# Layer 0, first block: GpSimd normalises ten of the eleven parts of x, and the zero fills of u come after its last part

## The chip, the cores and the metric

The kernel runs on one NeuronCore of a Trainium2 chip. The metric is the device time of one execution in microseconds; the time given for a kernel is the median of its runs. Engines are named as the profile names them: PE (TensorE matmuls), PEld (its weight loads), DVE (VectorE), ACT (ScalarE), POOL (GpSimd) and SP (SyncE, which here only issues DMAs). `L470` is line 470 of the kernel's source.

## The reference

Four residual layers follow one another on x of shape 4 x 64 x 256 x 256 (batch, channels, rows, columns), all in float32: `x = x + conv(group_norm(x))`. Only layer 0 is touched by the change:

```python
def _L0_conv_ref(x, w_in, w_dw, fft_filter, w_out):
    x = jnp.einsum('bchw,oc->bohw', x, w_in)
    ...
    xf = jnp.fft.rfft2(xp) * fft_filter
    xp = jnp.fft.irfft2(xf, s=(p, p))
    ...
    x = lax.conv_general_dilated(x, w_dw, window_strides=(1, 1), padding=[(1, 1), (1, 1)], feature_group_count=C)
    x1, x2 = jnp.split(x, 2, axis=1)
    x = jax.nn.gelu(x1, approximate=False) * x2
    return jnp.einsum('bchw,oc->bohw', x, w_out)
...
x = x + _L0_conv_ref(_gn(x), L0_conv_w_in, L0_conv_w_dw, L0_conv_fft_filter, L0_conv_w_out)
```

`_gn` is a group norm with 32 groups of two channels, so that a normalised value is `r * x + nb` with one r and one nb for each channel and image. `w_in` widens 64 channels to 384; the FFT filter acts in patches of 8 x 8; the depthwise convolution has zero padding at the image's edge; `w_out` brings 192 gated channels back to 64.

## The kernel before

**Blocks and parts.** Layer 0 goes through 12 blocks, three to an image, each with 11 rows of patches (`blocks`, `NR`). A row of patches of x is loaded as two parts of 128 partitions x 1024 elements (four image rows each); the last row of block 0 is loaded as a single part of the same size that holds all eight image rows. So block 0 has 11 parts, `first_parts[0]` to `first_parts[10]`. The first ten are already in SBUF when the statistics are done, because they are the last ten tiles over which the statistics of image 0 run (`kept`); part 10 is loaded afterwards (L424), into a buffer that a normalised part sets free.

**Before the first block.** PE builds small tables, DVE expands them (`tables`), ACT and POOL copy them into the tiles T (L390), and POOL stores T to DRAM as the weights wt (L394). In the same time DVE takes the statistics of image 0 (L317), and `group_norm` turns them into r and nb (L197 to L218, the power on POOL at L217). The tile u is then allocated in the memory of a pool that held T, so whatever writes u first has to wait until the stores of T have landed.

**Normalising a part** (`normalize_x`, L429): either ACT does it (`normalize`, L253) or POOL (`tensor_scalar`, L441). In every block but the first it is ACT alone.

**A block.** It has four rounds `kb` of 48 channels. A round first runs `expand` (L459) for each step: 16 matmuls (32 records in the profile, since each float32 matmul shows as two) multiply a row or half rows of x with `win` into two PSUM tiles, and these are copied to u by ACT (the first tile) and DVE (the second), four copies each in the form that round 0 uses (L486). There are four such PSUM tiles, so two steps are in flight. Block 0 has 11 steps. A step reads all eight image rows of its patches, so steps 2j and 2j+1 need parts 2j and 2j+1; step 10 needs part 10. After the steps, the round runs its convolution and patch filter as matmuls on u (`own` L523 and `beside` L539), then Gelu on ACT (L546), the product on DVE (L547) and a store to DRAM from POOL (L550).

**Zeros.** u has cells outside the image. `clear_sides` (L729) fills two edge columns, two inner columns and a tail with zeros; the loop at L765 fills the row above the image in block 0 (and a row in the other blocks at an image's edge). All of them are POOL memsets; no copy of `expand` writes the same cells, and the matmuls of `own` and `beside` read them.

**Order of the work.** Within layer 0 the order on PE, DVE, ACT and SP is that of the source (`manual_schedule`, L677); POOL is not in that list, and the order of its instructions is decided by the planner. In block 0, round 0, the source normalises parts 0 to 3 ahead of step 0 and then one part ahead of each of the steps 1 to 7 (L793 to L795), odd parts on POOL and even ones on ACT. The planner's order on POOL before is: power L217, memset L767 (the row of zeros), parts 1, 3, 5, the five memsets of `clear_sides`, parts 7 and 9, and then the stores of L550. On ACT before, parts 0 and 2 stand ahead of the copies of step 0, and parts 4, 6, 8 and 10 stand between the copies of the steps. SP's order is: the loads of the first weights (L498), part 10 (L424), one more weight, and then x of image 1 for its statistics (L668).

Of the kernel before, what the change touches and what calls it, by code (L numbers as in the profile page):

```python
# [13 lines left out]
ALU = mybir.AluOpType  # L14
# [104 lines left out]
class _Net:  # L119
# [152 lines left out]
    def _layer0(self, ctx, dst):  # L272
        tc, nc, a, B, H, W = self.tc, self.nc, self.a, self.B, self.H, self.W
        pool = lambda name, bufs, **k: ctx.enter_context(tc.tile_pool(name=name, bufs=bufs, **k))
# [11 lines left out]
        HC = W // P // 2 + 1  # L286
        CW = 2 * HC
# [4 lines left out]
        NR = 11  # L292
# [118 lines left out]
        def parts_of(p):  # L411

            b, i0 = blocks[p]
            out = [(b, i0 + 1 + 2 * m, k) for m in range(NR // 2) for k in range(2)]
            return out + ([(b, i0 + NR, 2)] if i0 + NR < NP else [])
# [13 lines left out]
        def normalize_x(part, pool=False):  # L429
            b, i, k = part  # L430
            x = x0.pop(part).rearrange("p r w -> p (r w)")
            if k == 2:
                xns[b, i] = p_x1.tile([128, HW2 // P, P, P], F32, tag="x1", name=f"xn_{b}_{i}")
            elif k == 0:
                xns[b, i] = p_xn.tile([128, W // P, P, P], F32, tag="xn", name=f"xn_{b}_{i}")
            to = xns[b, i].rearrange("p m r w -> p r m w")
            if k < 2:
                to = to[:, 4 * k : 4 * k + 4]
            x = x.rearrange("p (r m w) -> p r m w", r=P if k == 2 else 4, w=P)
            if pool:  # L440
                nc.gpsimd.tensor_scalar(to, x, self.r[0][:, b : b + 1], self.nb[0][:, b : b + 1], ALU.mult, ALU.add)  # L441
            else:
                self.normalize(to, x, 0, b)

# [3 lines left out]
        E1, O1, O2, E2 = 0, HC, 1, HC  # L448

        def steps_of(p):  # L450

            b, i0 = blocks[p]
            one = lambda t: [(b, i0 + t, 0, [(t, 0), (t, 1)])] if 0 <= i0 + t < NP else []
            out = one(0)
            for t in range(1, NR, 2):
                out += [(b, i0 + t, q, [(t, q), (t + 1, q)]) for q in range(2)]
            return out + one(NR)
# [146 lines left out]
        def load_half(p, r, half):  # L604
            if 0 <= p < NB and r < P:
                if half == 0 and (p, r) not in rts:
                    load_r(p, r)
                load_g(p, r, half)
# [73 lines left out]
        with ordered:  # L682

            bst0 = new_bst0(0)
            first_parts = parts_of(0)
# [35 lines left out]
            u = None  # L721
            ctx_u = ExitStack()
            u = ctx_u.enter_context(tc.tile_pool(name="l0u", bufs=1))
            u = u.tile([128, PB, (NR + 1) * CW + 2], F32, name="u")
            sources = []
            rows_u = u[:, :, 0 : (NR + 1) * CW].rearrange("p c (t w) -> p c t w", w=CW)
            lo, hi = halves

            def clear_sides():  # L729

                nc.gpsimd.memset(rows_u[lo, :, :, E1], 0.0)
                nc.gpsimd.memset(rows_u[lo, :, :, O1 + HC - 1], 0.0)
                nc.gpsimd.memset(rows_u[hi, :, :, 0], 0.0)
                nc.gpsimd.memset(rows_u[hi, :, :, E2], 0.0)
                nc.gpsimd.memset(u[:, :, (NR + 1) * CW :], 0.0)

            for p in range(NB + 1):
                units = iter([(r, half) for r in range(P) for half in range(2)] if p > 0 else [])
                ahead, first = 1, []
                if p == NB:  # L740
                    ctx_u.close()
                    sources.append([pool("l0g1e", 6), pool("l0g6e", 6), pool("l0re", 3)])
                    ahead = 3
                for r in range(ahead):
                    for half in range(2):
                        first.append((p - 1, r, half))
                        if p == NB:
                            load_half(*first.pop())

                def unit():  # L750
                    at = next(units, None)
                    if at:
                        project(p - 1, *at)
                        load_half(p - 1, at[0] + ahead, at[1])

                if p == NB:
                    for k in range(2 * P):
                        unit()
                    while self.norms:
                        self.next_norms()  # L760
                    break
                b, i0 = blocks[p]
                fresh = parts_of(p + 1) if p + 1 < NB else []
                steps = steps_of(p)
                for t in (0, NR):  # L765
                    if not 0 <= i0 + t < NP:
                        nc.gpsimd.memset(rows_u[:, :, t], 0.0)  # L767
                nk = [] if b + 1 >= B else list(range(p % NI * NJ // NI, (p % NI + 1) * NJ // NI))
                loaded, begun, coming = [], iter(fresh), iter(fresh)

                def load_next(kb):
                    if kb == 3:
                        load_rows(2)
                    elif nk:
                        loaded.append(nk.pop(0))
                        load_stats(b + 1, loaded[-1])

                def load_rows(n):
                    for _, row in zip(range(n), begun):
                        load_x(row)  # L780

                def normalize_rows(n):
                    for _, row in zip(range(n), coming):
                        normalize_x(row)
                    load_rows(n)

                for kb in range(4):
                    for t in range(NR + 1):
                        if p == 0 and kb == 0:
                            if t == 1:  # L790
                                for part in first_parts[len(kept) :]:
                                    load_x(part)
                            for n in range(4) if t == 0 else range(t + 3, t + 4):  # L793
                                if n < len(first_parts):
                                    normalize_x(first_parts[n], pool=n % 2 == 1)  # L795
                        if t < len(steps):
                            expand(p, kb, steps[t], kb == 0 or t < (NR + 1) // 2)
                        if t in (0, 4) and first:
                            load_half(*first.pop(0))
                        if t == NR:  # L800
                            load_w(p * (HID // 8) + NG * kb // 2 + 3)
                            load_next(kb)
                    if p == 0 and kb == 0:
                        clear_sides()
                        ctx_f.close()
                        p_1, p_6 = (pool(n, 2, side="right") for n in ("l0g1", "l0g6"))
                        sources.append([p_1, p_6, pool("l0r", 2, side="right")])
                    for g in range(0, NG, 2):
                        if g > 0:
                            load_w(p * (HID // 8) + (NG * kb + g) // 2 + 3)  # L810
                        if g in (0, 2, 6, 8):
                            unit()
                        if g < 6 and kb < 3:
                            load_next(kb)
                        if kb == 3 and g == 0:
                            assert not self.norms
                            normalize_rows(3)
                        for k in range(2):
                            own(p, kb, g + k)
                        for k in range(2):  # L820
                            beside(p, kb, g + k)
                        if g < NG - 2 or kb == 2:
                            self.next_norms()
                        if kb == 3:
                            normalize_rows(2)
                            if p == NB - 1 and g < 2 * (NR // 2):
                                load_r(p, g // 2)
                            continue
                        if loaded:
                            next_stats(b + 1, loaded.pop(0))  # L830
                        if kb == 2 and g == NG - 2:
                            load_rows(2)
                for t in range(NR):
                    xns.pop((b, i0 + t), None)
# [728 lines left out]
```

## Time and profile before

| | us |
|---|---|
| runs of the kernel before | 6346.17, 6347.42, 6354.44 |
| median | 6347.42 |
| the profiled execution's own time | 6345.01 |
| its span, first to last instruction | 6343.0 |
| ACT, 17 normalisations of 128 x 1024 up to 365 us (L253) | 1.224 to 1.242 each |
| POOL, 5 normalisations of 128 x 1024 (L441) | 1.184 to 1.199 each |
| POOL, memset of the row of zeros (L767) | 1.467 |
| POOL, memsets of `clear_sides` (L731 to L735) | 1.116, 1.197, 1.143, 1.192, 0.197 |
| ACT copy to u, round 0 of block 0 (L486, 44 of them) | 0.482 to 0.532 |
| DVE copy to u, the same round (44 of them) | 0.549 to 0.564 |

Times inside the profile are counted from the start of its span. A line of the timeline gives the start, the duration, engine, source line, operation and tiles, how many instructions are merged in it, and in brackets how long the engine was idle just before and what ended that. Lines of one engine can be merged over short gaps. Engines run side by side, so a busy engine matters only where another one waits for it. A line of the waits gives who waited for whom, in total, how often, and the longest. The chain is followed back from the last instruction through whatever released each step.

### The profile page before, as it was taken

What the parts mean: (1) busy time and instruction counts of PE and PEld (TensorE: products, weight loads), DVE (VectorE), ACT (ScalarE), POOL (GpSimd) and SP (SyncE); (2) the same over time, 40 slices, a digit from 0 to 9 for tenths busy, and PEclk for the clock granted to TensorE, in tenths of its full rate; (3) what the DMA queues carried; (4) which work ended last, traced back from release to release, by engine and by line L of the source; (5) the groups of instructions that cost most, each with busy time, mean ns of one, the idle gap of its engine ahead of it and who ended that gap; (6) DMA issues with size and microseconds to landing.
All of it is one profiled execution on the core that took longest, in us unless ns stands there. A gap on an engine that the chain in (4) does not pass through costs nothing.

```text
span 6343.0 us, 233229 instructions
## 1 busy us (share of the span) xinstructions
PE 5965.4 (94%) x104150; PEld 3328.8 (52%) x104150; DVE 4315.4 (68%) x6003; ACT 3274.7 (52%) x4639; POOL 1054.2 (17%) x1651
## 2 busy tenths in 40 slices
PE   3999999999999999999999969999899999999987
PEld 2565655566665655556665533333344444443566
DVE  6566666666666666656665549999788988984265
ACT  4454444445454444344544407777777777772111
POOL 4111111111111111111111111111122222221011
PEclk9999999999999999999999979999999999999755
DMA  7477888887887878887768799999566666678799
GB/s 221 157 209 220 241 240 248 244 235 228 239 234 225 239 231 241 235 249 207 219 200 224 217 239 246 227 230 225 136 175 174 175 173 176 175 189 292 290 374 393
DMA packets 769595, 1441.98 MB, mean 227 GB/s; under 512 B 77412, under 2 KB 463476, under 8 KB 766548
## 3 DMA queue, kind: packets, MB, share of 16 engines
q1 hardware_dynamic: 616388, 917.72, 54.7%
q0 software_dynamic: 148672, 500.14, 23.5%
q8 instruction: 823, 13.48, 0.9%
q10 hardware_dynamic: 3536, 9.20, 0.6%
q14 instruction: 176, 1.44, 0.1%
HBM read 926.71 MB, written 500.04 MB: 225 GB/s over the span
## 4 chain that ended last, share of the span: by engine, by line
PE 83%; DVE 6%; DMA 6%; ACT 3%; issue 2%; POOL 0%; SPq 0%; ACTq 0%; POOLq 0%; DVEq 0%
PE pc L539 18%; PE pc L523 12%; PE m L946 10%; PE one L1187 9%; PE psu L470 8%; PE div L1146 7%; PE po L632 4%; DVE u L486 4%; PE psu L476 3%; PE psz L1176 2%; PE po L639 2%; ACT u L486 2%; PE psy L1521 2%; PE psa L1374 2%; DMA x<-x 2%
## 5 line engine op out<-in xcount | busy, mean ns | idle before, releaser
L547 DVE TENSOR_TENSOR h<-h,pc 128x374 f32<-128x374 f32 x1152 | 575.4, 541 | 1168.8 <-ACT h L546 1168.8
L546 ACT ACTIVATE h<-pc 128x374 f32<-128x374 f32 x1152 | 493.4, 480 | 1682.3 <-PE pc L539 1682.3
L539 PE MATMUL pc<-u,w 64*16 64x374 f32 (+2 forms) x27648 | 1178.0, 479 | 4.7 <-issue 4.5
L550 POOL DMA_DIRECT2D g<-h x576 | 415.5, 721 | 2834.5 <-DVE h L547 2724.2
L523 PE MATMUL pc<-u,w 64*64 64x374 f32 x9216 | 832.0, 484 | 10.1 <-DVE u L490 3.4
L486 DVE COPY u<-psu 64x384 f32<-64x384 f32 x1408 | 782.3, 556 | 60.4 <-PE psu L470 36.4
L539 PEld LDWEIGHTS pc<-u,w 64*16 64x16 f32 (+2 forms) x27648 | 465.5, 92 | 682.0 <-issue 645.4
L470 PE MATMUL psu<-win,xn 64*128 64x96 f32 x11264 | 759.9, 277 | 47.7 <-ACT u L486 26.7
L486 ACT COPY u<-psu 64x384 f32<-64x384 f32 x1408 | 722.8, 513 | 128.2 <-PE psu L470 100.8
L470 PEld LDWEIGHTS psu<-win,xn 64*128 64x128 f32 x11264 | 714.4, 188 | 114.3 <-ACT u L486 36.2
L1132 DVE TENSOR_TENSOR q<-xn 128x2313 f32<-128x2313 f32 (+2 forms) x256 | 628.0, 2495 | 1.7 <-ACT xn L253 1.7
L1187 PE MATMUL one<-z,wp 32*32 32x512 f32 x16384 | 598.1, 598 | 18.7 <-issue 14.9
L253 ACT ACTIVATE xn<-x,nb,r 128x1024 f32<-128x1024 f32 (+3 forms) x267 | 475.3, 1802 | 179.2 <-DMA x<-r 117.8
L523 PEld LDWEIGHTS pc<-u,w 64*64 64x64 f32 x9216 | 363.9, 132 | 383.5 <-issue 159.1
L1133 ACT ACTIVATE q<-q 128x2313 f32<-128x2313 f32 (+2 forms) x256 | 529.2, 2087 | 31.4 <-DVE q L1132 30.3
L1187 PEld LDWEIGHTS one<-z,wp 32*32 32x32 f32 x16384 | 368.7, 103 | 228.2 <-issue 87.7
L1146 PE MATMUL div<-q,ones 64*32 64x512 f32 x8192 | 465.9, 596 | 11.1 <-ACT q L1133 9.5
L1220 POOL DMA_DIRECT2D x<-r x512 | 274.5, 544 | 974.7 <-DVE r L1217 959.5
L476 PE MATMUL psu<-win,xn 64*64 64x96 f32 x12288 | 345.6, 250 | 39.9 <-issue 18.4
L632 PE MATMUL po<-g,wo 128*64 128x176 f32 (+1 forms) x3072 | 315.2, 348 | 45.0 <-DMA g<-g 36.9
L476 PEld LDWEIGHTS psu<-win,xn 64*64 64x64 f32 x12288 | 299.8, 135 | 82.3 <-issue 34.5
L946 PE MATMUL m<-t,wk 64*64 64x512 f32 x3072 | 341.1, 588 | 0.0
(157 smaller groups left out, 6428.7 us busy)
## 6 DMA issues: line engine op xcount, KB each, us to landing
g<-h POOLq DMA_DIRECT2D x576, 374.0 KB, 6.7
x<-x SPq DMA_DIRECT2D x240, 640.0 KB, 6.5
w<-wt SPq DMA_DIRECT2D x288, 448.0 KB, 6.9
x<-x SPq DMA_DIRECT2D x100, 1024.0 KB, 14.1
g<-g SPq DMA_DIRECT2D x414, 187.0 KB, 6.4
g<-g SPq DMA_DIRECT2D x736, 93.5 KB, 6.0
x<-in_x_dram SPq DMA_DIRECT2D x256, 256.0 KB, 8.0
x<-o POOLq DMA_DIRECT2D x128, 512.0 KB, 8.3
```

Of the source, the lines that this page charges most:

```text
L470: nc.tensor.matmul(ps[s][:, k, at], xn[halves[s], n : n + 2].rearrange("p n r w -> p (n r w)"), win[halves[s], kb, 0 : 2 * PB], start=True ...
L476: nc.tensor.matmul(ps[s][halves[1 - odd], k, at], xn[halves[s], n + odd].rearrange("p r w -> p (r w)"), win[halves[s], kb, PB * (1 - odd) ...
L486: copy(at(h, o0 + o), v[k, c : c + PB])
L523: nc.tensor.matmul(out(C * c, C, k, h), w[halves[h], k, 2 * (G % 2) + c, 0:C], cells(h, 4 * g + 2 * k + c, 0, 0), start=True, stop=False, ...
L539: nc.tensor.matmul(out(q, m, k, h), w[halves[h], k, 2 * (G % 2) + c, c0 : c0 + m], cells(h, 4 * g + 2 * k + c, down, right), start=False, ...
L547: nc.vector.tensor_mul(h[:, k], h[:, k], ps[k][:, 1, 0:L])
L632: nc.tensor.matmul(out(k, s, x), wo1, moving(g1[:, 2 * k], 2 * half + k, s, x), start=(x == 0), stop=False, skip_group_check=True,)
L946: nc.tensor.matmul(rows2(m)[halves[j], s], w[dx][halves[s]], ts[n][halves[s], i, 2 * j : 2 * j + 2, dx : dx + W], start=(dx == 0), stop=(d ...
L1132: nc.vector.tensor_sub(d, p0, p1)
L1133: nc.scalar.activation(d, d, AF.Square)
L1146: ins = nc.tensor.matmul(ps[quarters[j], h], ones[halves[h]], q[n, g, k][halves[h], r + 2 * j : r + 2 * j + 2, o : o + W], start=(m == 0), ...
L1187: ins = nc.tensor.matmul(rows2(ps[g])[quarters[j], k], w[quarters[i]], z[quarters[i], h, 2 * j + dy : 2 * j + dy + 2, dx : dx + W], tile_p ...
```

## The change

In block 0, round 0, POOL normalises parts 1 to 10 and ACT only part 0; they are still called in the same order from the same places. `normalize_x` hands back the POOL instruction. The row of zeros of block 0 is no longer filled at the head of the block: it joins the fills of `clear_sides` after round 0's steps, and each of these six memsets gets an added dependency on the last POOL normalisation, that of part 10. In the other blocks the row fills stay where they were.

The planner's order on POOL is then: power L217, parts 1 to 10 in turn, the memset of the row, the tail, the four columns, and then the stores. ACT's instructions lose parts 2, 4, 6, 8 and 10 and keep their order otherwise. The orders on PE, DVE and SP are as before. The buffer for part 10 is one that POOL's normalisations set free, where it was ACT's before; the loads of L668 follow with the other buffers. PE's step 10 waits for POOL as well, and PE's first matmul of `own` waits for POOL's memsets.

```diff
--- before.py
+++ after.py
@@ -438,7 +438,7 @@
                 to = to[:, 4 * k : 4 * k + 4]
             x = x.rearrange("p (r m w) -> p r m w", r=P if k == 2 else 4, w=P)
             if pool:
-                nc.gpsimd.tensor_scalar(to, x, self.r[0][:, b : b + 1], self.nb[0][:, b : b + 1], ALU.mult, ALU.add)
+                return nc.gpsimd.tensor_scalar(to, x, self.r[0][:, b : b + 1], self.nb[0][:, b : b + 1], ALU.mult, ALU.add)
             else:
                 self.normalize(to, x, 0, b)
 
@@ -728,11 +728,8 @@
 
             def clear_sides():
 
-                nc.gpsimd.memset(rows_u[lo, :, :, E1], 0.0)
-                nc.gpsimd.memset(rows_u[lo, :, :, O1 + HC - 1], 0.0)
-                nc.gpsimd.memset(rows_u[hi, :, :, 0], 0.0)
-                nc.gpsimd.memset(rows_u[hi, :, :, E2], 0.0)
-                nc.gpsimd.memset(u[:, :, (NR + 1) * CW :], 0.0)
+                at = [rows_u[lo, :, :, E1], rows_u[lo, :, :, O1 + HC - 1], rows_u[hi, :, :, 0], rows_u[hi, :, :, E2]]
+                return [nc.gpsimd.memset(v, 0.0) for v in at + [u[:, :, (NR + 1) * CW :]]]
 
             for p in range(NB + 1):
                 units = iter([(r, half) for r in range(P) for half in range(2)] if p > 0 else [])
@@ -762,11 +759,18 @@
                 b, i0 = blocks[p]
                 fresh = parts_of(p + 1) if p + 1 < NB else []
                 steps = steps_of(p)
+                zero_rows = []
                 for t in (0, NR):
                     if not 0 <= i0 + t < NP:
-                        nc.gpsimd.memset(rows_u[:, :, t], 0.0)
+                        zero_rows.append(t)
                 nk = [] if b + 1 >= B else list(range(p % NI * NJ // NI, (p % NI + 1) * NJ // NI))
                 loaded, begun, coming = [], iter(fresh), iter(fresh)
+
+                def clear_rows():
+                    return [nc.gpsimd.memset(rows_u[:, :, t], 0.0) for t in zero_rows]
+
+                if p > 0:
+                    clear_rows()
 
                 def load_next(kb):
                     if kb == 3:
@@ -792,7 +796,7 @@
                                     load_x(part)
                             for n in range(4) if t == 0 else range(t + 3, t + 4):
                                 if n < len(first_parts):
-                                    normalize_x(first_parts[n], pool=n % 2 == 1)
+                                    last = normalize_x(first_parts[n], pool=n > 0)
                         if t < len(steps):
                             expand(p, kb, steps[t], kb == 0 or t < (NR + 1) // 2)
                         if t in (0, 4) and first:
@@ -801,7 +805,8 @@
                             load_w(p * (HID // 8) + NG * kb // 2 + 3)
                             load_next(kb)
                     if p == 0 and kb == 0:
-                        clear_sides()
+                        for ins in clear_rows() + clear_sides():
+                            self.after(ins, last)
                         ctx_f.close()
                         p_1, p_6 = (pool(n, 2, side="right") for n in ("l0g1", "l0g6"))
                         sources.append([p_1, p_6, pool("l0r", 2, side="right")])
```

## The prediction

> **What bounds the kernel now.** I read the page first, then the timeline of the first 145 us, where all of block 0's round 0 lies, then the waits there and the same stretch in block 1. Over the whole span PE is the busy engine:
>
> ```profile
> PE 5965.4 (94%) x104150; PEld 3328.8 (52%) x104150; DVE 4315.4 (68%) x6003; ACT 3274.7 (52%) x4639; POOL 1054.2 (17%) x1651
> ```
>
> The edit touches one of the few places where PE is not busy. The timeline shows two losses there, a late start and a slow pace:
>
> ```profile
> 100.13 2.37 ACT L253 ACTIVATE xn<-x,nb,r 128x1024 f32<-128x1024 f32 x2 [18.59 <-DVE nb L218]
> 104.34 1.47 POOL L767 MEMSET u<- 128x1632 f32 x1 [4.43 <-DMA w<-wt]
> 105.80 3.54 POOL L441 TENSOR_SCALAR xn<-x,r,nb 128x1024 f32<-128x1024 f32 x3
> 107.04 5.62 PE L470 MATMUL psu<-win,xn 64*128 64x96 f32 x64 [7.98 <-POOL xn L441]
> 110.90 6.85 DVE L486 COPY u<-psu 64x384 f32<-64x384 f32 x12 [10.80 <-PE psu L470]
> ...
> 114.26 4.27 ACT L486 COPY u<-psu 64x384 f32<-64x384 f32 x8
> 118.56 1.24 ACT L253 ACTIVATE xn<-x,nb,r 128x1024 f32<-128x1024 f32 x1
> 118.57 4.56 DVE L486 COPY u<-psu 64x384 f32<-64x384 f32 x8 [0.82 <-PE psu L470]
> 119.83 4.27 ACT L486 COPY u<-psu 64x384 f32<-64x384 f32 x8
> 124.12 1.24 ACT L253 ACTIVATE xn<-x,nb,r 128x1024 f32<-128x1024 f32 x1
> 124.14 4.56 DVE L486 COPY u<-psu 64x384 f32<-64x384 f32 x8 [1.00 <-PE psu L470]
> ...
> 135.22 4.60 DVE L486 COPY u<-psu 64x384 f32<-64x384 f32 x8 [0.96 <-PE psu L470]
> ```
>
> The start: r and nb are known at 100.10 and ACT begins part 0 at once, but POOL's queue has the row memset in front of part 1, and that memset stands until 104.34 for a transfer. Part 1 starts at 105.80, and PE's first step at 107.04. The chain names the transfer as the last store of T, issued at 89.52 and landed 14.46 us later, at 103.98; the timeline's "w<-wt" is only what landed last by its guess.
>
> The pace: on ACT, eight copies (two steps) and one normalisation alternate, 118.56 to 124.12, 5.56 us for two steps. DVE is idle 0.8 to 1.0 us in each such pair, and PE waits for ACT. What the pace is without normalisations is seen in block 1, round 0, whose ACT has only copies: the DVE copies of the last 11 of its 12 steps are one line without a gap.
>
> ```profile
> 380.73 25.24 DVE L486 COPY u<-psu 64x384 f32<-64x384 f32 x44 [0.21 <-PE psu L470]
> ```
>
> That is 25.24 / 11 = 2.295 us a step, set by four DVE copies.
>
> Whether an earlier PE start is worth anything depends on when u's memory is free. The copies themselves wait for the stores of T too; the queue's own record of ACT says when that was over:
>
> ```profile
> L486 ACTq EVENT_SEMAPHORE  x1: 6528/6528/6528, 104.3 to 104.3; - x1
> ```
>
> At 104.3 ACT had passed all earlier waits of its first copy and stood 6.5 us longer for the last, PE. So the stores free u for everybody at about 104.35, not only for POOL.
>
> What follows is PE alone:
>
> ```profile
> 139.40:180.00 40.60, 40.60 (x766) 17.12 (x768) 16.18 (x31) 10.73 (x25) 7.46 (x11) 1.00 0.56 179
> ```
>
> From 139.4 to 180 PE (first pair of numbers) is busy for the whole 40.60 us. What is gained ahead of it moves it all.
>
> [...] 1.187 us on POOL against 1.240 on ACT for one part. [...] The DVE copies read PSUM; all 44 take 0.549 to 0.564 us, those beside POOL's two normalisations at 113.90 to 116.28 included. [...] step 0's 32 records take 3.78 us, a later step's 2.1. PE starts cold after the change too.
>
> **The change, part by part.**
>
> *Start.* Part 1 becomes POOL's first work after the power: from about 100.15 to 101.34. ACT's part 0 is the first half of the 2.37 us, to 101.37. PE then starts at 101.42, with the 0.05 us that it took before (part 1 ended at 106.99), which is 107.04 - 101.42 = 5.6 us earlier. Step 0 cold takes 3.8 us, so the first copies can start at 105.2, after u is free (104.35, 0.85 us to spare). Before it was 110.84 on ACT, 110.90 on DVE.
>
> *Pace.* Five normalisations leave ACT: part 2, which stood ahead of the steps and hid under the wait for part 1 (nothing), and parts 4, 6, 8, 10 at 1.24 us each. ACT's four copies take 2.13 us a step, DVE's 2.28, so DVE now sets the pace, 2.295 as in block 1. The eleven steps took 139.82 - 110.90 = 28.92 us from DVE's first copy to the end of its last; now 25.24. Gain 3.7 us, less than 4 x 1.24 = 4.96, because DVE is late next. Sum: 5.6 + 3.7 = 9.3 us, with DVE's last copy at 105.25 + 25.24 = 130.5 in place of 139.82.
>
> *POOL's load.* Ten parts at 1.187 us run from 100.15 to 112.0. Step 2j needs part 2j+1: part 3 at 103.7 for a step 2 that starts at about 107.5, part 9 at 110.8 for step 8 at about 121, and the margin grows. Part 10's load is issued once a POOL part frees its buffer, at 101.4 (ACT's part 0 freed one then); its two halves landed 5.5 to 6.1 us after issue, by 108.2, before POOL reaches it. If the buffer is part 3's it is 2.3 us later, and still in time. On SP only one weight and the loads of L668 stand behind it; those had waited until 107.01 for POOL's part 1 and can come sooner, and no engine waits for them before 147.
>
> *Zero fills.* Six memsets, 1.47 + 1.12 + 1.20 + 1.14 + 1.19 + 0.20 = 6.3 us, now follow part 10, from 112.0 to 118.4, or 119 with the waits. Their added wait is on POOL's own last normalisation; behind them are only POOL's stores, the first of which follows a product of DVE at about 136. Who needs them is `own` on PE at 137.34 - 9.3 = 128.0. Nine us of cover; once used up, each further us costs one.
>
> *Table load and the rest.* ACT's 1.28 us table load for Gelu at 139.44 stays hidden under `own` and moves with it.
>
> The profiled execution took 6345.01 for a span of 6343.0; its span should become 6333.7. The median of the runs is 2.4 above its time; from the median, 6347.42 - 9.3 = 6338.1, that is 0.15% less. 0.2%, 12.7 us, is about what a measurement of this kernel can tell from no change, so this counts as within it.
>
> **Unknowns.** [...] warm at once would bring the copies to 104.35 and save 0.9 more; cold through step 1 costs about 1[...]. So 8.3 to 10.2, with 9.3 as the same 3.8 us again. A slow landing of T's last store eats the start: from 105.2 on, one for one. Carrying through the other 6200 us I take as full: nothing in them depends on a fixed moment.
>
> **Rivals.**
> - *The start is held by the stores of T instead.* A transfer wait takes the place of POOL's. It decides past 105.2, 1.2 us later than the landing seen, and at 110.8 nothing of the 5.6 us is left: 6347.42 - 3.7 = 6343.7. For it: the DMA engines were 99% busy from 100 to 107. Against: nothing ahead of 101 is changed.
> - *Only the start gains*, because something other than ACT keeps the pace at 2.78: 6341.8. Block 1 speaks against it.
> - *Slower: the zero fills end last.* POOL's ten normalisations in a row could be slower than five in two groups. With t for each, the fills end at 106.9 + 10 t; they delay `own` from t = 2.1 us (128.0), cancel the gain at 3.0, and make the kernel 0.2% slower at t = 4.3, 6360.1. For it: everything is in one in-order queue. Against: 1.184 to 1.199 with DVE idle and with DVE busy.
> - *The gain is larger than 0.2%*: 9.3 us and 3.5 more, from the spread of two medians (the runs of before span 8.3 us) or from later waits that the shift closes; about 6333. Nothing in the profile points to such a wait.
>
> **Chances.** Forecast 0.67, stores 0.06, only the start 0.05, larger 0.17, slower fills and the like 0.05. Medians scatter by some 3 us, so of the forecast's cases about a tenth pass 12.7 us. Faster 0.24, within 0.70, slower 0.06. Range: 6331 to 6345, from the larger gain to the partial ones.
>
> **What would show it.** Right: POOL's part 1 at 100.2 and PE's first step at 101.4; DVE's 44 copies of round 0 as a nearly gapless line from 105.2 to 130.5; POOL's last memset before 120; `own` at 128; the span at about 6334. Wrong: PE waiting for POOL at a later step or at `own`; copies that start with T's stores and not with PE; POOL normalisations far above 1.2 us; or the 9.3 us present at 180 us and gone later.

## The result, and the profile after

| | before | after |
|---|---|---|
| median, us | 6347.11 (22 runs) | 6336.16 (22 runs) |
| lowest and highest, us | 6334.0 and 6356.99 | 6328.53 and 6349.62 |
| ratio, with its 95% interval | | 0.9985 (0.9979 to 0.9992) |
| span of the profiled execution, us | 6343.0 | 6346.7 |

The change makes the kernel 0.15% faster (0.08 to 0.21%), 9.5 us by the ratio (the two medians of the table lie 10.95 us apart, inside the same interval of 5 to 13); the forecast was 9.3 and 6338.1. The profiled execution of the changed kernel is one of its longer ones (own time 6348.79 against a median of 6336.16), so the two spans say nothing on the change. What it did is read in its stage, the first 140 us. The timeline of the changed kernel there, PE, DVE, ACT and POOL lines around round 0 of block 0:

```profile
101.19 1.24 ACT L253 ACTIVATE xn<-x,nb,r 128x1024 f32<-128x1024 f32 x1 [20.14 <-DVE nb L218]
101.27 11.77 POOL L441 TENSOR_SCALAR xn<-x,r,nb 128x1024 f32<-128x1024 f32 x10 [0.30 <-DVE nb L218]
102.53 8.77 PE L470 MATMUL psu<-win,xn 64*128 64x96 f32 x96 [2.42 <-POOL xn L441]
106.37 2.27 DVE L486 COPY u<-psu 64x384 f32<-64x384 f32 x4 [5.21 <-PE psu L470]
109.58 22.96 DVE L486 COPY u<-psu 64x384 f32<-64x384 f32 x40 [0.94 <-PE psu L470]
...
113.09 1.47 POOL L770 MEMSET u<- 128x1632 f32 x1
114.50 4.58 POOL L732 MEMSET u<- 128x96 f32 x5
...
132.09 2.81 PE L523 MATMUL pc<-u,w 64*64 64x374 f32 x28 [0.89 <-ACT u L486]
```

POOL's ten parts are one line that begins with r; the row of zeros (L770) and the five other fills (L732, all on that line now) follow and end at 119.08. PE's first step starts 1.34 us after ACT's part 0 and no longer 6.91. DVE's 44 copies are two lines, with a gap of 0.94 us between the first four and the other forty. `own`'s long batch, which stood at 139.37, stands at 132.09: 7.3 us earlier in span time, although this execution had r 1.06 us later than the profile before (part 0 at 101.19 against 100.13). How the next line of the windows reads: length, busy time and instructions of PE, PEld, DVE, ACT and POOL, granted clock, DMA share, GB/s.

```profile
132.00:180.00 48.00, 47.43 (x873) 23.66 (x874) 22.45 (x43) 16.64 (x36) 8.76 (x12) 1.00 0.61 190
```

PE is busy 47.43 of the 48 us that follow: what came in earlier is not given back there.

### The profile page after: what moved, and what is told of

It is laid out like the page before. It is cut to its first block, busy times and chain, and to the rows that moved or that the text cites. A ratio compares the mean times of both kernels' runs of the same rounds, so it can differ in the third digit from the quotient of the medians.

```text
span 6346.7 us, 233225 instructions
## 1 busy us (share of the span) xinstructions
PE 5964.6 (94%) x104150; PEld 3326.9 (52%) x104150; DVE 4314.4 (68%) x6003; ACT 3268.6 (52%) x4634; POOL 1059.9 (17%) x1656
## 4 chain that ended last, share of the span: by engine, by line
PE 81%; DVE 7%; DMA 6%; ACT 3%; issue 2%; SPq 0%; POOL 0%; ACTq 0%; POOLq 0%; DVEq 0%
PE pc L539 18%; PE pc L523 12%; PE m L951 10%; PE one L1192 9%; PE psu L470 8%; PE div L1151 7%; DVE u L486 4%; PE po L632 4%; PE psu L476 3%; DMA x<-x 3%; PE psz L1181 2%; PE po L639 2%; PE psa L1379 2%; DMA g<-g 1%; ACT u L486 1%
## 5 line engine op out<-in xcount | busy, mean ns | idle before, releaser
L523 PE MATMUL pc<-u,w 64*64 64x374 f32 x9216 | 831.1, 483 | 10.2 <-DVE u L490 3.3
L470 PEld LDWEIGHTS psu<-win,xn 64*128 64x128 f32 x11264 | 717.5, 188 | 103.9 <-DVE h L547 30.7
```

Of the source, the lines that this page charges most:

```text
L470: nc.tensor.matmul(ps[s][:, k, at], xn[halves[s], n : n + 2].rearrange("p n r w -> p (n r w)"), win[halves[s], kb, 0 : 2 * PB], start=True ...
L523: nc.tensor.matmul(out(C * c, C, k, h), w[halves[h], k, 2 * (G % 2) + c, 0:C], cells(h, 4 * g + 2 * k + c, 0, 0), start=True, stop=False, ...
```

## The experiments

All of them are judged by the stage, since the runs of one kernel spread over some 20 us, and a kernel of this section without a time was run once, beside one run of before. The moments of each profile that matter, in us from the span's start (the stores of T: when the queue of DVE had all its waits for its first copy behind it but the one for PE):

| run | ACT's part 0 | stores of T | first DVE copy | 44 DVE copies take | `own`, long batch |
|---|---|---|---|---|---|
| before | 100.13 | 104.4 | 110.90 | 28.92 | 139.37 |
| before, again | 98.59 | 104.1 | 110.59 | 28.94 | 139.08 |
| after | 101.19 | 103.9 | 106.37 | 26.17 | 132.09 |
| after, again | 99.48 | 104.0 | 104.66 | 26.16 | 130.37 |
| after, with the timed runs | 99.86 | 105.6 | 105.67 | 25.28 | 130.50 |
| the start alone | 98.44 | 104.0 | 104.11 | 28.90 | 132.56 |
| the share alone | 97.41 | 104.4 | 110.97 | 25.69 | 136.21 |
| 6 fills more | 99.86 | 106.8 | 106.86 | 27.51 | 133.91 |
| 14 fills more | 96.25 | 104.0 | 104.12 | 27.50 | 135.83 |
| 15 small matmuls ahead | 99.49 | 103.9 | 104.92 | 25.84 | 130.31 |
| 22 small matmuls ahead | 99.94 | 105.1 | 105.19 | 26.15 | 130.89 |
| 70, the long warm-up | 101.54 | 105.0 | 105.11 | 25.25 | 129.91 |
| the long warm-up, with the timed runs | 98.21 | 103.6 | 103.70 | 25.26 | 128.51 |

**The start alone.** Against the changed kernel:

```diff
+                last = None
...
-                                    last = normalize_x(first_parts[n], pool=n > 0)
+                                    last = normalize_x(first_parts[n], pool=n % 2 == 1) or last
```

> The start alone: the row of zeros leaves the head of GpSimd's queue and all fills follow GpSimd's last part, while the parts stay shared as before (odd on GpSimd, even on ScalarE). Measured inside the profile, from the start of ScalarE's part 0 to the start of the long batch of own: 39.24 us before, 30.90 after the change. My theory (the gain is a start and a pace that add up): first VectorE copy at +5.2 as after the change, pace still 5.56 us for two steps, so own at about 33.6 to 34.6 (5.6 gained, up to 1 lost to a cold TensorE). Rival (the share alone makes the gain, an early start is lost again in waiting for ScalarE): own at about 38 to 39.

The timeline of this kernel:

```profile
98.44 2.37 ACT L253 ACTIVATE xn<-x,nb,r 128x1024 f32<-128x1024 f32 x2 [16.28 <-DVE nb L218]
99.78 6.15 PE L470 MATMUL psu<-win,xn 64*128 64x96 f32 x64 [2.42 <-POOL xn L441]
104.11 6.85 DVE L486 COPY u<-psu 64x384 f32<-64x384 f32 x12 [5.70 <-DMA wt<-T]
...
111.73 1.24 ACT L253 ACTIVATE xn<-x,nb,r 128x1024 f32<-128x1024 f32 x1
111.74 4.55 DVE L486 COPY u<-psu 64x384 f32<-64x384 f32 x8 [0.78 <-PE psu L470]
117.32 1.24 ACT L253 ACTIVATE xn<-x,nb,r 128x1024 f32<-128x1024 f32 x1
...
132.56 2.81 PE L523 MATMUL pc<-u,w 64*64 64x374 f32 x28 [0.89 <-DVE u L486]
```

`own` at 34.1 us after part 0, inside what I gave. The pace is the old one: 117.32 - 111.73 = 5.59 us for two steps, and 28.90 for all 44 copies. So moving the row of zeros behind the parts is worth 6.5 to 6.8 us in this execution, by itself. But the reason that the first copy came at +5.7 and not at +5.2 is in the bracket of the DVE line: it ended a wait for T's store. PE had step 0 ready at 103.5. The rival to which I had given 6 in 100, copies held by the stores, was real here, at a cost of 0.5 us (5.67 us after part 0 and not 5.18).

**The share alone.** The change without its added waits:

```diff
-                        for ins in clear_rows() + clear_sides():
-                            self.after(ins, last)
+                        clear_rows()
+                        clear_sides()
```

> The share alone: the change without the six added waits, after which the planner puts the row of zeros back at the head of GpSimd's queue, in front of part 1; GpSimd still has parts 1 to 10. My theory: TensorE's first step stays at +6.9 us from ScalarE's part 0 and the first copy at +10.8, then 2.3 us a step without gaps, so own at about 35.6 (3.7 gained), up to 36.6 if TensorE stays cold through step 1. Rival (the order of GpSimd's queue is of no account, what counts is ScalarE's relief): own at about 31, as after the change.

Its timeline:

```profile
97.41 1.24 ACT L253 ACTIVATE xn<-x,nb,r 128x1024 f32<-128x1024 f32 x1 [15.39 <-DVE nb L218]
104.42 1.47 POOL L770 MEMSET u<- 128x1632 f32 x1 [7.24 <-DMA x<-in_x_dram]
105.87 11.77 POOL L441 TENSOR_SCALAR xn<-x,r,nb 128x1024 f32<-128x1024 f32 x10
107.11 8.30 PE L470 MATMUL psu<-win,xn 64*128 64x96 f32 x96 [10.78 <-POOL xn L441]
110.97 2.26 DVE L486 COPY u<-psu 64x384 f32<-64x384 f32 x4 [13.60 <-PE psu L470]
113.71 22.95 DVE L486 COPY u<-psu 64x384 f32<-64x384 f32 x40 [0.48 <-PE psu L470]
...
136.21 2.80 PE L523 MATMUL pc<-u,w 64*64 64x374 f32 x28 [0.89 <-ACT u L486]
```

The pace gained 28.93 - 25.69 = 3.2 us and `own` stands 3.0 us ahead of the mean of the two profiles before (139.22), so the two halves are about 6.6 and 3.1. They add up to 9.7 us, more than the 8.2 that three profiles of the whole change show in the mean: each half is one execution, and in that of the start alone part 0 came early, at 98.44. The rival falls: with the planner's own order of POOL's queue the row of zeros is back in front and part 1 waits behind it. My number, +35.6 after part 0, missed (+38.8), and it was the yardstick: part 0 came early, at 97.41, and the row of zeros at 104.42 all the same. What begins with that memset hangs on the stores of T and not on r. The next run puts that to the test.

**Both kernels once more.** No edit.

> The kernel before once more, for the moment at which the stores of T land. In the runs so far ScalarE's part 0 started anywhere from 96.2 to 101.2 us from the span's start, while the stores of T landed close to 104 in all. New theory (before the change the start hangs on the stores alone): the row of zeros starts at 104.0 to 104.6, TensorE's step 0 2.7 us later, own's long batch at 139.0 to 139.9, whatever part 0 does. Rival (it hangs on r and nb): own 39.2 us after part 0, wherever that falls.

> The changed kernel once more. New theory (the first copy starts at the later of two: part 0 + 5.2 us, or the landing of T's stores near 104.1): the first VectorE copy at that moment, own's long batch 25.3 to 26.3 us later, so between 129.4 and 132.5 in span time, and in an execution with part 0 ahead of 98.9 the copies start with the stores and not with TensorE. Rival (only the first of the two counts, as I forecast): first copy always 5.2 us after part 0.

The timeline of the kernel before, then that of the changed one:

```profile
98.59 2.37 ACT L253 ACTIVATE xn<-x,nb,r 128x1024 f32<-128x1024 f32 x2 [16.92 <-DVE nb L218]
104.03 1.47 POOL L767 MEMSET u<- 128x1632 f32 x1 [5.66 <-DMA x<-in_x_dram]
106.73 5.56 PE L470 MATMUL psu<-win,xn 64*128 64x96 f32 x64 [9.21 <-POOL xn L441]
110.59 6.86 DVE L486 COPY u<-psu 64x384 f32<-64x384 f32 x12 [12.03 <-PE psu L470]
...
139.08 2.81 PE L523 MATMUL pc<-u,w 64*64 64x374 f32 x28 [0.95 <-DVE u L486]
```

```profile
99.48 1.24 ACT L253 ACTIVATE xn<-x,nb,r 128x1024 f32<-128x1024 f32 x1 [18.15 <-DVE nb L218]
100.82 8.76 PE L470 MATMUL psu<-win,xn 64*128 64x96 f32 x96 [2.42 <-POOL xn L441]
104.66 2.26 DVE L486 COPY u<-psu 64x384 f32<-64x384 f32 x4 [5.22 <-PE psu L470]
107.86 22.96 DVE L486 COPY u<-psu 64x384 f32<-64x384 f32 x40 [0.94 <-PE psu L470]
...
130.37 2.80 PE L523 MATMUL pc<-u,w 64*64 64x374 f32 x28 [0.90 <-ACT u L486]
```

With part 0 at 98.59 and not 100.13, the kernel before started its copies only 0.31 earlier, as the stores landed 0.3 earlier: its start hung on the stores, and `own` stood at 139.08, where the new theory had it. The changed kernel's copies came at part 0 + 5.18, as the forecast had it; and 28.9 us of copies have become 26.16 and not 25.24, because of the same gap of 0.94. A third profile of it, taken with the timed runs at the end, shows the other case, stores that land late:

```profile
99.86 1.24 ACT L253 ACTIVATE xn<-x,nb,r 128x1024 f32<-128x1024 f32 x1 [17.03 <-DVE nb L218]
101.20 27.26 PE L470 MATMUL psu<-win,xn 64*128 64x96 f32 x352 [2.42 <-POOL xn L441]
105.67 25.28 DVE L486 COPY u<-psu 64x384 f32<-64x384 f32 x44 [5.84 <-DMA wt<-T]
...
130.50 2.81 PE L523 MATMUL pc<-u,w 64*64 64x374 f32 x28 [0.89 <-ACT u L486]
```

> The changed kernel, timed beside it on the same chip: a ratio of 0.9985 as measured before, own's long batch 25.3 to 26.3 us after the first VectorE copy unless the stores of T land after 105.2.

There the copies start with the store (the bracket of the DVE line says "DMA wt<-T" again) 0.7 us after PE has step 0 ready, at 104.93, and then run without a gap: step 1 was slow here too (3.22 us), but PE did it while the copies waited. Timed, it gives 6334.87 us (21 runs) against 6344.44 of before (33 runs), a ratio of 0.9985 (0.9979 to 0.9992), as in the first table.

**More fills.** The row of zeros filled k times more behind the last part, k = 14 and k = 6; only zeros in cells that are zero already.

```diff
+                        extra = [nc.gpsimd.memset(rows_u[:, :, 0], 0.0) for _ in range(k)]
-                        for ins in clear_rows() + clear_sides():
+                        for ins in clear_rows() + clear_sides() + extra:
```

> The change, with the row of zeros filled 14 times more behind GpSimd's last part (same zeros, same cells). After the change the fills end at +17.9 us from ScalarE's part 0 and own starts at +28.8 with its first matmul, so there are 10.9 us of cover. Theory (fills are free only under that cover): 14 fills of about 1.42 us end at about +38, so own's long batch starts at +38 to +38.5 in place of +30.9, that is 7 to 7.6 later, which uses up the gain nearly whole. Rival (TensorE doesn't really wait for the fills, or the fills also slow VectorE's copies): own at +30.9, or VectorE's copies above 0.56 us.

> The change with the row of zeros filled 6 times more behind GpSimd's last part. By the cover of 10.9 us the 6 fills of 1.42 us (8.5 us, ending at about +26.5 from ScalarE's part 0) cost nothing: own's long batch 25.3 to 26.3 us after the first VectorE copy, TensorE not waiting for GpSimd. Rival (any work on GpSimd beside the copies slows them): later than that, with VectorE copies above 0.56 us.

The timeline of the run with 14 fills:

```profile
107.35 1.19 POOL L441 TENSOR_SCALAR xn<-x,r,nb 128x1024 f32<-128x1024 f32 x1 [0.43 <-DMA x<-in_x_dram]
...
131.49 4.29 POOL L732 MEMSET u<- 64x576 f32 x4
133.65 1.50 PE L523 MATMUL pc<-u,w 64*64 64x374 f32 x2 [4.52 <-POOL u L732]
135.83 4.83 PE L523 MATMUL pc<-u,w 64*64 64x374 f32 x30 [0.67 <-POOL u L732]
```

With 14 fills PE stood 4.52 us for POOL at `own`, and the long batch started 0.05 us after the last fill ended (131.49 + 4.29 = 135.78): `own` waits for the fills once the cover is gone, as forecast. It came at +39.6 and not at +38 to +38.5, as part 10 was 0.43 us late from DRAM and one fill followed another every 1.52 us (13 in 19.77; a single one takes 1.467, as before the change), where I had reckoned 1.42. With 6 fills the last ended at 122.78 + 4.41 = 127.19 and `own` began at 131.80 without a wait for POOL, so they cost nothing by themselves. Yet `own` came 27.05 us after the first copy and not within 26.3, which none of my cases had. VectorE's copies were not slower (0.556 us in the mean). The timeline and the windows of the run with 6 fills show what it was:

```profile
101.20 5.66 PE L470 MATMUL psu<-win,xn 64*128 64x96 f32 x64 [2.42 <-POOL xn L441]
106.86 4.56 DVE L486 COPY u<-psu 64x384 f32<-64x384 f32 x8 [7.03 <-PE psu L470]
108.97 8.76 PE L470 MATMUL psu<-win,xn 64*128 64x96 f32 x96 [2.11 <-POOL xn L441]
...
113.01 2.26 DVE L486 COPY u<-psu 64x384 f32<-64x384 f32 x4 [1.59 <-PE psu L470]
```

```profile
105.00:109.00 4.00, 1.89 (x33) 1.75 (x31) 2.10 (x4) 2.15 (x5) 4.00 (x4) 0.94 1.11 256
109.00:113.00 4.00, 4.00 (x37) 4.00 (x38) 2.34 (x5) 2.24 (x5) 3.63 (x4) 0.50 0.91 215
```

In this execution the stores landed at 106.8. PE finished two steps, both pairs of PSUM tiles were full, and PE stood idle for 2.11 us (the bracket names POOL's parts; those were done long before, and what PE waited for was the first copies). After that its granted clock was 0.50 from 109 to 113, and step 2, about 2 us at full clock (1.96 in the first profile of the change), took 3.91. The run with 14 fills shows the same, with PE idle for 2.55 us and a step 2 of 3.91. So in these two runs, whose stores landed 1.9 and 2.7 us after step 0 was ready, the stores cost twice: the wait, and a step 2 of 3.91 us in place of 1.96.

**Warm-up.** The last question was the gap of 0.94 us. In the profiles after, step 1's matmuls take 3.2 to 3.5 us; in the profiles before, 2.0 to 2.1. The suspect is a TensorE still slow after its idle time, as it was at step 2 of the run with 6 fills (granted clock 0.50 after 2.11 us idle); "cold" and "up" in the expectations stand for steps at the slow and at the fast time. The windows can't tell: they print a clock of 1.00 for steps 0 and 1 too, because the trace has no record of the clock from that time. Its first record is a stretch at full clock, and the start of that stretch fits the steps: 3.8 and 3.7 us after PE began step 0 in the two profiles before, at the end of step 0, but 6.7, 6.7 and 6.1 us in the three after, inside step 1. Small matmuls in PE's idle time ahead of step 0, their results unused, were to test whether steps 0 and 1 then take 2 us. Three sizes: 15 of 128 x 96 on the whole array, 22 of step 0's own form, and 70 of that form, 54 of them in one go and from an earlier moment on. The edit with 70, where `keep_warm(n)` (not shown) issues n of them:

```diff
-            self.group_norm(0, 0, bst0)
+            keep_warm(54)
+            for k, _ in enumerate(self.group_norm_parts(0, 0, bst0)):
+                if k == 1:
+                    keep_warm(4)
+            keep_warm(12)
```

> The change, with 15 small matmuls of 128 x 96 on TensorE (results not used) in the time in which it stands idle ahead of step 0: 8 ahead of the first matmul of the group norm, 1 between its two, 6 behind. Theory (the 1 us by which the gain fell short of 9.3 is the cold array at steps 0 and 1): step 0 takes about 2.1 us in place of 3.8, step 1 is no longer late, the first copy comes at +3.4 to +4.2 (the second if the stores of T hold it), and own at about +28.3 to +29.1. Rival (the shortfall is something else, such as the wait for PSUM or for the stores): own at +30.9 as after the change, or later by what the small matmuls delay the group norm.

> The change, with 22 matmuls of the very form of step 0 (64 rows of x by 128 with 96 columns of win, on the two row halves in turn, results not used) ahead of step 0: 12 ahead of the first matmul of the group norm, 2 between its two, 8 behind. With 15 matmuls of 128 x 96 on the full array step 0 stayed slow (3.8 us) and the array came up only 6 us later. Theory (those did not count as load, matmuls of step 0's form do): step 0 takes about 2.1 us, steps follow without the 0.9 us gap of VectorE, first copy at the later of part 0 + 3.5 and 104.1, own's long batch 24.8 to 25.2 us after it. Rival (what lies ahead of step 0 doesn't bring the array up because of the gaps around the group norm): step 0 at 3.8 us as in the change.

> The change, with 70 matmuls of step 0's form ahead of step 0 (results not used): 54 without a pause from about 87 us on, 4 between the two matmuls of the group norm, 12 behind them. 22 of them, with pauses, left step 0 at 3.73 us and step 1 at 3.50. Theory (the array needs a longer stretch without pauses, and the 0.94 us gap of VectorE between its first and second four copies is a cold step 1): the array is up before 97, step 0 takes about 2.1 us, step 1 as well, no gap of VectorE above 0.3, and the first copy comes at the later of part 0 + 3.5 and the landing of T's stores (103.6 to 104.7 in most runs). own's long batch then 24.8 to 25.2 us after the first copy, against 25.7 in the change. Rival (the pauses of the group norm throw the array back): step 0 at 3.73, gap as before.

The first two brought nothing: step 0 took 3.73 us in both, step 1 3.15 and 3.50, and the gaps of DVE stayed (0.63 and 0.93). With the 15, PE had no pause above 0.12 us from 93.12 to the end of step 2, and the record of full clock still starts only at 107.10, in step 1. The timeline with 70:

```profile
88.31 9.61 PE L725 MATMUL warm<-win,x 64*128 64x96 f32 x106 [0.69 <-DMA x<-in_x_dram]
...
101.54 1.24 ACT L253 ACTIVATE xn<-x,nb,r 128x1024 f32<-128x1024 f32 x1 [19.69 <-DVE nb L218]
102.92 3.81 PE L470 MATMUL psu<-win,xn 64*128 64x96 f32 x64 [0.95 <-POOL xn L441]
105.11 25.25 DVE L486 COPY u<-psu 64x384 f32<-64x384 f32 x44 [3.61 <-PE psu L470]
107.22 20.64 PE L470 MATMUL psu<-win,xn 64*128 64x96 f32 x288 [0.49 <-issue]
...
129.91 2.81 PE L523 MATMUL pc<-u,w 64*64 64x374 f32 x28 [0.90 <-ACT u L486]
```

Steps 0 and 1 together take 3.81 us (2.03 and 1.98), the first copy comes 3.6 us after part 0 and not 5.2, and all 44 copies are one line of 25.25 us, the 25.24 that the forecast had taken from block 1. `own` comes 28.4 us after part 0; in the two executions of the changed kernel whose copies PE started it is 30.9. The record of full clock starts at 95.35 here, ahead of step 0. So the gap came from the slow step 1, and with both steps at 2 us `own` comes 2.5 us earlier when the stores of T allow it (they landed at 105.0, just as step 0 was ready). Why 15 or 22 matmuls did not do is open: length, start and pauses were changed together.

> The change with the long warm-up, timed. From the stage (own's long batch 2.5 us earlier than in the change when part 0 starts at the same moment) I expect 9.5 + 2.5 = 12 us under the kernel before, a ratio of 0.9981, with an interval too wide to tell it from the change alone. Rival (the warm-up costs as much at the group norm as it brings at step 0): the ratio of the change, 0.9985, or above.

Timed, this version has 6329.84 us (13 runs) and a ratio to before of 0.9979 (0.9970 to 0.9987). It has the lowest median of the kernels that were timed, and its interval overlaps that of the change: that it is faster than the change is shown in the stage only. The profile taken with these runs also shows a slow step 0 behind the same warm-up: part 0 came at 98.21, step 0 took 3.52 us, but the stores held the copies until 103.70 anyway, which then ran without a gap (25.26). The granted clock was 0.50 there, as the windows of that profile show:

```profile
99.87:103.28 3.41, 3.41 (x37) 3.41 (x35) 0.00 (x0) 0.00 (x0) 3.41 (x4) 0.50 0.85 236
```

## Why the prediction was right

*Start.* Forecast 5.6 us. PE's first step came 1.34 us after part 0 in all three profiles of the change (forecast 1.29), step 0 took 3.73 (3.8), the first copy came at +5.18 where PE decided. Against the mean of the two profiles before (110.75), the first copies after are 4.4, 6.1 and 5.1 us earlier, 5.2 in the mean. The mechanism was right, its yardstick not quite: I moved PE's start by a fixed amount, but before the change it hangs on the stores of T, and after it PE hangs on r, and the copies on the later of PE and the stores. From one execution to the next r moves by 5 us (part 0 at 96.25 to 101.54), the stores by 2.9 (103.9 to 106.8), so the gain differs from run to run.

*Pace.* Forecast 3.7 us. ACT's four normalisations between the copies are gone and DVE sets the pace at 2.295 us a step, as read from block 1. The gain was 2.8, 2.8 and 3.7. The missing 0.9 is the term that the unknowns had: "cold through step 1 costs about 1", an estimate of mine that no trace of before showed. I took the value without it. Step 1 was slow in all three profiles, at 3.2 to 3.5 us against 2.1 before; two of them lost the time, in a gap of 0.94 us, and in the third the copies waited for the stores anyway.

*Sum.* In the stage, 139.22 against 130.99 for the mean of the three: 8.2 us, below the 9.3 and just under my bounds of 8.3 to 10.2. The times give 9.5 with an interval of 5 to 13, which agrees with both. That the 9.5 comes so near to my 9.3 is luck: by the stage I was about 1 us too high.

*POOL's load, fills and table load.* Ten parts at 1.184 to 1.195 us (forecast 1.187), done 11.85 us after the start of part 0; part 10 in time in every profile of the change. The fills ended at +17.9 (forecast 118.4 to 119, which is +18.3 to +18.9), `own` needed them at +28.8 (+27.9): 10.9 us of cover where I had 9. The 14 fills showed what lies behind the cover: `own` starts with the end of the fills, as the rival "fills end last" had it. ACT's table load (132.02 in the first profile, 1.28 us) stayed under `own`.

*Copies beside GpSimd.* VectorE's copies took 0.555 to 0.556 us in the mean in every run, with POOL reading and writing SBUF next to them, and 0.556 in block 1 of the kernel before, where POOL is busy for 0.00 us during the 25.24 us of copies from 380.73 on: they were not slower beside POOL. These copies read PSUM; no run has copies that read SBUF there.

*Stores of T.* This is where the chances were off. I gave the rival 0.06, as an all-or-nothing case, though my unknowns had it as one for one from 105.2 on. The stores did decide the first copy in one of three profiles of the change, with both sizes of fills, and with the start alone, so a sign that I had named for being wrong, copies that start with T's stores, did appear; they cost 0.5 to 2.7 us each time (first copy less part 0 + 5.18), never the 5.6.

*Carried through.* The gain of the stage agrees with the times. At 180 us, matched matmul by matmul, the three profiles of the change lie within 1.8 us of one another and 8.2 us in the mean ahead of the two before. Further on it can't be followed in single executions: the three lie within 12 us of one another at 3600 and within 20 at 6200.

*What 0.2% means.* I called 12.7 us about what a measurement can tell; 22 runs of each kernel told 9.5 from nothing.

## What to carry to other kernels

Look at what stands at the head of an in-order queue when the critical value arrives: a zero fill that waited for its memory held POOL's first part of x, and with it TensorE, for 5.6 and 6.8 us in the two profiles before. When work leaves an engine, price the gain by the engine that is late next, and find that pace in a stretch of the same kernel where the work is absent; here 25.24 us from block 1 came back as 25.25 to 25.28 wherever no slow step of PE made a gap. Where a start depends on two things, such as statistics and a transfer, ask for each kernel which of the two it hangs on, and look at more than one execution before you take their distance as fixed.

## What the runs showed of the hardware

- In the kernel before, the trace's first record of full clock starts 3.8 and 3.7 us after the start of step 0, in the changed kernel 6.7, 6.7 and 6.1 us. Step 0's 32 records took 3.73 us in every profile but those of the long warm-up, where they took 2.03 and 3.52, and step 1's anything from 1.98 to 3.50. Work on TensorE ahead of step 0 did not by itself change that: 22 matmuls of step 0's form in the 9 us ahead, with pauses of 0.4 to 0.7 us, left steps 0 and 1 at 3.73 and 3.50, and with 15 of 128 x 96 without a pause above 0.12 us the record of full clock starts only 14 us after the first of them. Why is open.
- After idle stretches of only 2.11 and 2.55 us between two steps, step 2 took 3.91 us in place of 1.96, with a granted clock of 0.50 from 109 to 113 in the run with 6 fills. After the gaps of 1.1 to 1.3 us that the kernel before had in each pair of steps, the pair took 4.2 to 4.3 us, no more than 2.2 a step. The length of the gap doesn't decide alone: in the timed long warm-up the clock was at 0.50 from 99.87 after a pause of 0.95 us, and in the other profile of the same kernel step 0 took 2.03 us after a pause of 0.95 us.
- One program of fixed work on one core spread from 6326 to 6346 us in 21 runs on one chip. Little of it arises early: three profiles of that kernel lie within 1.8 us of one another at 180 us.
